# Second layer of a two-layer AdaLN model: positive parts and normalisation on ScalarE, inverse roots on GpSimd, key tiles in pairs, one output scaling per tile

## The chip, the cores and the metric

The kernel runs on one core of a Trainium2 chip. A core has TensorE (PE, matmuls), VectorE (DVE), ScalarE (ACT), GpSimd (POOL) and SyncE (SP, here only the issue of DMAs), each with an instruction queue of its own that is worked off in order. The metric is device time in microseconds (us), the median of several runs. All data are float32.

## The reference

Two layers, each an attention and a mixture of experts, both with a layer norm that is scaled and shifted per batch. x has four batches of 1024 rows of 256 columns. The change touches the second layer's attention and the routing of its experts. Cut to that:

```python
h = _layernorm(x) * (1 + ca) + sa
q, k, v = split(h @ w_qkv.T)                  # 16 heads of 16
q = norm(norm(relu(q) + 1e-6) ** 3)           # norm: t / t.sum(-1)
k = norm(norm(relu(k) + 1e-6) ** 3)
kv = einsum('bhnd,bhne->bhde', k, v)
z = 1 / (einsum('bhnd,bhd->bhn', q, k.sum(2)) + 1e-6)
out = einsum('bhnd,bhde,bhn->bhne', q, kv, z)
out = out + conv3(out) + b_dwc                # three taps along the rows
x = x + ga * (out @ w_proj.T + b_proj)
h = _layernorm(x) * (1 + cb) + sb
logits = h @ router_w + router_b              # 8 experts, the largest is taken
x = x + gb * gate * (h @ expert_w[idx] + expert_b[idx])
```

## The kernel before, in words

x stays on the chip, one tile of 128 partitions by eight row tiles by 256 columns for each batch. The first layer's attention, its experts, the second layer's attention and its experts follow one another. The second attention (`attention1`) starts while the last two batches of the first experts are still being put together (`combine`: `out` is scaled by ScalarE, gets its second term on VectorE, is multiplied by the gate on GpSimd and added to x on VectorE).

`attention1` works batch by batch. `front(b)` takes the layer norm (`layer_norm_steps`: statistics and inverse root, normalised rows `ln_xn`, transposes into `ps_lnT`, scaled and shifted into `hT`), then the keys and values: for each row tile a product `ps_k`, its positive part plus 1e-6 (`r`), the cube (`k3`, shown as k), the reciprocal of the head's sum (`recs`), and the values times that reciprocal (`v`, with the reciprocal itself as a 17th column of each head). The product `ps_kv` of k and v is issued two row tiles late, through the list `waiting`. Then four tiles of queries `ps_q` are cubed into `qT`. `back(b)` multiplies qT with the summed kv (`ps_o`), divides (`on`), transposes (`ps_oT`, `o`), applies the three taps (`y`), projects (`ps_pr`) and adds to x. The bias is added to x on GpSimd beforehand (the 128x1024 addition of `bg`).

Steps of `front(b)` and `back(b-1)` alternate, and with each step `Around` spends a credit on work beside: first `combine`, then the routing `route` of batches whose attention is done (`row_statistics`, and `routed_rows`: normalise, scale and shift into `h`, transpose, multiply with the router's weights, turn the result). Ranks and lists follow (`ps_rank`, `ps_list`), and GpSimd scatters the rows to the experts' places (`sorted`). The gate's products `scaled` for the final sum stand on GpSimd too. The last batch is routed in two halves of four tiles. In this part of the kernel a scheduler orders the instructions of each engine; the order is fixed when the kernel is built, and every engine keeps to it.

An inverse root is either `rsqrt` (13 small instructions on VectorE, three Newton steps) or `power` (an addition and a power on GpSimd).

PSUM has eight banks: three for `ps_p` (ps_k, ps_q), three for `ps_m` (ps_lnT, ps_o, ps_oT, ps_pr and the routing's), two for the sums of kv.

Of the kernel before, what the change touches and what calls it, by code (L numbers as in the profile page):

```python
# [8 lines left out]
F32 = mybir.dt.float32  # L9
# [99 lines left out]

def layer_norm_T(k, b, hT, layer, which, psum, psum_tag):  # L110
    for _ in layer_norm_steps(k, b, hT, layer, which, psum, psum_tag, k.work):
        pass


def layer_norm_steps(k, b, hT, layer, which, psum, psum_tag, xn_pool):
# [13 lines left out]
    rsqrt(nc, pool, rstd, mv[:, :, 1], NT, LN_EPS)  # L129
    yield 1.5  # L130
    for q in range(2):
        xn = xn_pool.tile([P, 4, C], F32, tag="ln_xn", name="ln_xn", bufs=k.xn_bufs)
        for i in range(4):
            t = 4 * q + i
            nc.vector.tensor_scalar(
                xn[:, i, :], k.x[b][:, t, :], mv[:, t, 0:1], rstd[:, t : t + 1],
                ALU.subtract, ALU.mult,
            )
        yield 1.5
        for cc in range(CC):  # L140
            yield BANK
            ps = psum.tile([P, 512], F32, tag=psum_tag, name="ps_lnT")
            for i in range(4):
                nc.tensor.transpose(
                    ps[:, i * P : (i + 1) * P], xn[:, i, cc * P : (cc + 1) * P], k.ident
                )
            scale = k.modT[layer][:, 6 * which + 2 + cc, b : b + 1]
            shift = k.modT[layer][:, 6 * which + cc, b : b + 1]
            dst = hT[:, cc, q * 512 : (q + 1) * 512]
            if cc == 0:  # L150
                nc.vector.tensor_scalar(dst, ps, scale, shift, ALU.mult, ALU.add)  # L151
            else:
                nc.scalar.activation(dst, ps, AF.Identity, bias=shift, scale=scale)
            yield 0.7
# [919 lines left out]
def routed_rows(k, work, b, t0, nt, h, mv, rstd, scale, shift, wr):  # L1074
# [3 lines left out]
    for q in range(0, nt, 4):  # L1078
        for i in range(q, q + 4):
            nc.vector.scalar_tensor_tensor(  # L1080
                h[:, i, :C], k.x[b][:, t0 + i], mv[:, i, 0:1], scale, ALU.subtract, ALU.mult
            )
            nc.vector.scalar_tensor_tensor(
                h[:, i, :C], h[:, i, :C], rstd[:, i : i + 1], shift, ALU.mult, ALU.add
            )
            yield 0.9
# [375 lines left out]
def attention1(ctx, k, a, after_rows=lambda b, t, n: None):  # L1462
# [6 lines left out]
    ps_p = ctx.enter_context(k.tc.tile_pool(name="a1_ps_p", bufs=3, space=PSUM, reuse_waits="tile"))  # L1469
    ps_m = ctx.enter_context(k.tc.tile_pool(name="a1_ps_m", bufs=3, space=PSUM, reuse_waits="tile"))  # L1470
# [27 lines left out]
    same = same.rearrange("p (h d) -> p h d", d=D)  # L1498
    kvs, qTs = {}, {}

    recs = wp.tile([P, 2, B, NT, H], F32, tag="recs", name="recs")

    def front(b):
# [13 lines left out]
        for t in range(NT):  # L1517
            ps = ps_p.tile([P, 512], F32, tag="p", name="ps_k")
            for cc in range(CC):
                nc.tensor.matmul(  # L1520
                    ps, lhsT=hT[:, cc, t * P : (t + 1) * P], rhs=wqkv[:, cc, C:],
                    start=cc == 0, stop=cc == CC - 1,
                )
            r = work.tile([P, C], F32, tag="r", name="r", bufs=3)
            nc.vector.tensor_scalar(r, ps[:, :C], 0.0, 1e-6, ALU.max, ALU.add)  # L1525
            k3 = work.tile([P, C], F32, tag="k3", name="k3", bufs=3)
            nc.scalar.activation(k3, r, AF.Square)  # L1527
            nc.gpsimd.tensor_tensor(k3, k3, r, ALU.mult)
            rk = recs[:, 0, b, t]
            nc.vector.tensor_reduce(rk, k3.rearrange("p (h d) -> p h d", d=D), AX.X, ALU.add)  # L1530
            nc.vector.reciprocal(rk, rk)
            v = work.tile([P, H, D + 1], F32, tag="v", name="v", bufs=3)
            nc.gpsimd.tensor_copy(v[:, :, D], rk)  # L1533
            nc.vector.tensor_tensor(  # L1534
                v[:, :, :D], ps[:, C:].rearrange("p (h d) -> p h d", d=D), bcast(rk, 2, D), ALU.mult
            )
            waiting.append((t, k3, v))
            if len(waiting) > 2:
                product(*waiting.pop(0))
            yield  # L1540

        qT = qTs[b] = work.tile([P, CC, N], F32, tag="qT", name="qT")
        for cc in range(CC):
            for q in range(2):
                cols = slice(q * 512, (q + 1) * 512)
                ps = ps_p.tile([P, 512], F32, tag="p", name="ps_q")
# [6 lines left out]
                nc.vector.tensor_scalar(r, ps, 0.0, 1e-6, ALU.max, ALU.add)  # L1553
                nc.scalar.activation(qT[:, cc, cols], r, AF.Square)
                nc.gpsimd.tensor_tensor(qT[:, cc, cols], qT[:, cc, cols], r, ALU.mult)
# [15 lines left out]
    def back(b):  # L1571
# [10 lines left out]
        for q in range(2):  # L1582
            on = work.tile([P, 4, C], F32, tag="on", name="on")
            for i in range(4):
# [9 lines left out]
                for cc in range(CC):  # L1594
                    nc.vector.tensor_tensor(
                        on[:, i, cc * P : (cc + 1) * P].rearrange("p (h d) -> p h d", d=D),
                        ps[:, cc, :P].rearrange("p (h d) -> p h d", d=D),
                        bcast(z[:, cc], 2, D), ALU.mult,
                    )
# [201 lines left out]
class Experts1:  # L1801
# [24 lines left out]
    def route(self, block):  # L1826
# [7 lines left out]
        mv, rstd = yield from row_statistics(k, self.work, b, t0, nt, rsqrt)  # L1834
# [4 lines left out]
        tr = yield from routed_rows(k, self.work, b, t0, nt, h, mv, rstd, scale, shift, self.wr)  # L1839
# [299 lines left out]
```

## Time and profile before

| | |
|---|---|
| time, median of 3 runs (lowest to highest) | 1149.53 us (1149.14 to 1150.41) |
| profiled execution: its own time, its span | 1181.49 us, 1179.8 us |
| mean granted TensorE clock of that execution | 0.897 |
| busy over the span: PE, DVE, ACT, POOL | 943.3, 642.7, 513.4, 476.8 us |
| first layer norm instruction of the second attention | about 768 us |
| first ps_k, last ps_pr of the second attention | 780.7 us, about 1038 us |
| first transpose of an expert's tile after it | 1065.5 us |

The profiled execution is one execution, with the profiler on, and takes 32 us more than the median. In the profile a line such as L1525 is a line of the kernel; a fp32 matmul shows as two records; what ends an engine's idle time is named after it. Idle time of an engine that nobody waits for costs nothing.

### The profile page before, as it was taken

Reading aid. Unit: us, or ns where it says so; the run is one execution under the profiler, and the core shown is the slowest. Engines: PE = TensorE matmul, PEld = TensorE weight load, DVE = VectorE, ACT = ScalarE, POOL = GpSimd, SP = SyncE. Lnnn points to the kernel's source line nnn. Section 1 sums busy time; section 2 is a strip of 40 time slices with the busy share of each in tenths; the row PEclk is TensorE's granted clock in tenths of the full one; section 3 lists DMA queues with packets and bytes.
Section 4 is the critical chain, followed back from the end, with each engine's and each line's share of the span. In section 5 each row is a group of like instructions: output and inputs, shape, how many; then the busy total and the mean of one; then the engine's idle time right before and its main releaser. Section 6 shows DMA issues by size and latency. Waiting matters only on the chain.

```text
span 1179.8 us, 18176 instructions
## 1 busy us (share of the span) xinstructions
PE 943.3 (80%) x5920; PEld 546.9 (46%) x5920; DVE 642.7 (54%) x1971; ACT 513.4 (44%) x777; POOL 476.8 (40%) x714
## 2 busy tenths in 40 slices
PE   5699999999999988796879989636787888646750
PEld 3443434434434433234758878413544554434640
DVE  4351336324624464324656656588895877772263
ACT  0148765776686554563546656521213131211110
POOL 0012212222542374431465556765244425443561
PEclk9789999999999998897989998767898999868875
DMA  6200000000100042317235334353001001014455
GB/s 223 81 14 2 1 1 6 5 1 1 50 33 1 10 152 99 125 56 277 90 132 173 124 100 145 109 161 125 1 5 41 1 10 40 6 59 152 148 193 170
DMA packets 62726, 92.18 MB, mean 78 GB/s; under 512 B 9170, under 2 KB 53144, under 8 KB 61857
## 3 DMA queue, kind: packets, MB, share of 16 engines
q1 hardware_dynamic: 51488, 64.88, 17.1%
q0 software_dynamic: 10272, 25.24, 6.0%
q8 instruction: 50, 0.82, 0.3%
q10 hardware_dynamic: 864, 0.82, 0.2%
q14 instruction: 52, 0.42, 0.1%
HBM read 58.02 MB, written 35.76 MB: 79 GB/s over the span
## 4 chain that ended last, share of the span: by engine, by line
PE 47%; DVE 18%; POOL 12%; issue 11%; DMA 5%; ACT 3%; SPq 1%; another core or an unknown queue 1%; DVEq 0%; POOLq 0%; ACTq 0%
PE ps_s L425 12%; PE ps_av L498 11%; POOL results L1114 5%; PE ps_q L409 3%; PE ps_out L469 2%; PE ps_pr L1625 2%; PE ps_mod L170 2%; PE ps_h L1302 2%; DMA xs<-sorted 2%; POOL sorted L1062 2%; DMA wmod<-in_wmod_dram 1%; PE ps_lat L362 1%; DMA ys<-results 1%; PE ps_lnT L1092 1%; PE ps_rows L184 1%
## 5 line engine op out<-in xcount | busy, mean ns | idle before, releaser
L433 ACT ACTIVATE pT<-ps_s 128x1024 f32<-128x1024 f32 x288 | 278.9, 1022 | 135.4 <-PE ps_s L425 121.8
L436 POOL TENSOR_SCALAR_AFFINE_SELECT pT<-pT 128x256 f32<-128x256 f32 x256 | 100.7, 415 | 282.6 <-ACT pT L433 278.2
L425 PE MATMUL ps_s<-qT,kT 32*128 32x512 f32 (+3 forms) x1536 | 178.5, 529 | 4.4 <-ACT pT L433 4.4
L498 PE MATMUL ps_av<-pT,v 128*32 128x512 f32 (+3 forms) x1536 | 168.3, 500 | 7.7 <-DVE sq L447 5.8
L1062 POOL DMA_INDIRECT sorted<-h,index x96 | 96.7, 1007 | 62.6 <-DVE ln_rstd L99 26.4
L425 PEld LDWEIGHTS ps_s<-qT,kT 32*128 32x128 f32 x1536 | 74.6, 185 | 101.5 <-issue 73.2
L1114 POOL DMA_INDIRECT results<-y,ids x79 | 80.1, 1014 | 55.3 <-DVE y L1366 38.1
L1350 ACT ACTIVATE act<-ps_hT,gain 128x128 f32<-128x128 f32 x158 | 59.4, 456 | 66.4 <-PE ps_hT L1346 52.6
L498 PEld LDWEIGHTS ps_av<-pT,v 128*32 128x32 f32 x1536 | 41.6, 109 | 98.3 <-issue 55.6
L1361 PE MATMUL ps_y<-w,act 128*128 x316 | 81.9, 405 | 1.8 <-ACT act L1350 1.8
L1302 PE MATMUL ps_h<-w,xT 128*128 x316 | 79.4, 396 | 0.6 <-issue 0.3
L447 DVE STREAM_TRANSPOSE sq<-ps_av 128x512 f32<-128x512 f32 x32 | 22.8, 713 | 100.4 <-PE ps_av L498 100.4
L1520 PE MATMUL ps_k<-wqkv,hT 128*128 128x512 f32 x128 | 70.0, 675 | 6.2 <-DVE hT L151 6.2
L1361 PEld LDWEIGHTS ps_y<-w,act 128*128 128x128 f32 x316 | 63.6, 204 | 12.7 <-ACT act L1350 3.1
L1302 PEld LDWEIGHTS ps_h<-w,xT 128*128 128x128 f32 x316 | 59.3, 198 | 9.3 <-issue 1.2
L1307 DVE TENSOR_TENSOR hid<-ps_h,b 128x256 f32<-128x256 f32 x79 | 33.5, 424 | 45.5 <-PE ps_h L1302 34.7
L1114 POOL DMA_INDIRECT results<-y,xs x39 | 38.0, 975 | 39.6 <-DVE y L1911 26.8
L1905 PE MATMUL ps_y<-we,xT 128*128 x156 | 45.3, 442 | 10.5 <-ACT xT L1900 8.2
L1334 ACT ACTIVATE hid<-hid,nmr,rstd 128x256 f32<-128x256 f32 x79 | 43.7, 611 | 11.3 <-DVE nmr L1324 11.3
L1511 PE MATMUL ps_kv<-v,k 128*128 128x136 f32 x128 | 23.0, 305 | 31.0 <-DVE v L1534 24.6
L1511 PEld LDWEIGHTS ps_kv<-v,k 128*128 128x128 f32 x128 | 19.9, 206 | 53.5 <-POOL v L1533 44.6
L1527 ACT ACTIVATE k<-r 128x256 f32<-128x256 f32 x32 | 13.3, 417 | 71.2 <-DVE r L1525 35.3
(233 smaller groups left out, 1645.0 us busy)
## 6 DMA issues: line engine op xcount, KB each, us to landing
xs<-sorted SPq DMA_DIRECT2D x118, 128.5 KB
w<-in_w_dram SPq DMA_DIRECT2D x8, 1024.0 KB
ys<-results SPq DMA_DIRECT2D x32, 256.0 KB
x<-in_x_dram SPq DMA_DIRECT2D x4, 1024.0 KB
b<-in_b_dram SPq DMA_DIRECT2D x2, 2048.0 KB
ys<-results SPq DMA_DIRECT2D x8, 512.0 KB
out_dram<-x SPq DMA_DIRECT2D x8, 512.0 KB
sorted<-fill SPq DMA_DIRECT2D x26, 128.5 KB
```

What stands on the lines that cost most here:

```text
L425: nc.tensor.matmul(pair[hh // 2][:, hh % 2, c0 : c0 + w], lhsT=kTs[o][rows, kb * P : (kb + 1) * P], rhs=qT[rows, q1 - w : q1], start=True, ...
L433: nc.scalar.activation(pT, ps, AF.Exp, scale=1.0 / L**0.5)
L436: nc.gpsimd.affine_select(out=pT[:, :, c0 : c0 + P], in_=pT[:, :, c0 : c0 + P], compare_op=ALU.is_ge, fill=0.0, base=0, pattern=[[0, 2], [ ...
L498: nc.tensor.matmul(po[32 * hh : 32 * hh + 32, 512 - w :], lhsT=vs[b % 2][:, kb, at : at + 32], rhs=exps[n, u][hh // 2][:, hh % 2, c0 : c0 ...
L1062: i = self.k.nc.gpsimd.indirect_dma_start(out=self.buffer.ap, out_offset=bass.IndirectOffsetOnAxis(ap=index, axis=0), in_=rows, in_offset= ...
L1114: k.nc.gpsimd.indirect_dma_start(out=buffer.ap, out_offset=bass.IndirectOffsetOnAxis(ap=ids, axis=0), in_=y, in_offset=None, bounds_check= ...
L1302: nc.tensor.matmul(ph[:, j], lhsT=st.xT[:, j, cc], rhs=w1[:, cc, bass.ds(st.at[j], C)], start=cc == 0, stop=cc == CC - 1,)
L1334: nc.scalar.activation(st.h[:, j], st.h[:, j], AF.Identity, bias=st.nmr[:, at : at + 1], scale=st.rstd[:, at : at + 1],)
L1350: nc.scalar.activation(st.act[:, j, cc], pt[:, j, cc], AF.Gelu, bias=gain[:, 1, cc, t : t + 1], scale=gain[:, 0, cc, t : t + 1],)
L1361: nc.tensor.matmul(po[:, j], lhsT=st.act[:, j, cc], rhs=w2[:, cc, bass.ds(st.at[j], C)], start=cc == 0, stop=cc == CC - 1,)
L1520: nc.tensor.matmul(ps, lhsT=hT[:, cc, t * P : (t + 1) * P], rhs=wqkv[:, cc, C:], start=cc == 0, stop=cc == CC - 1,)
L1905: nc.tensor.matmul(po[:, j], lhsT=xT[:, j, cc], rhs=we[:, cc, bass.ds(at[j], C)], start=cc == 0, stop=cc == CC - 1,)
```

## The change

- The second layer's layer norm: `power` on GpSimd in place of `rsqrt` on VectorE. The rows are normalised by ScalarE (`normal_rows`: a small product `nmr` of minus the mean and the root on VectorE, then one Identity with scale and bias for each row tile). All of hT is written by ScalarE.
- The routing: the same root and the same `normal_rows`, then for four row tiles together a product with the scale on VectorE and an addition of the shift on GpSimd.
- Keys: two row tiles share one two-bank PSUM tile. The positive part (Relu), the addition of 1e-6 (Identity with the bias `tiny`) and the square are three ScalarE instructions, the last product stays on GpSimd (`cubed`). Sum, reciprocal and values are one instruction each for the pair, and the reciprocal is copied into v by ScalarE. Queries use `cubed` too.
- `on`: one product for a row tile's 16 heads in place of two.
- PSUM: `ps_p` has two tiles of two banks, `ps_m` two of one bank.

```diff
+def normal_rows(k, pool, dst, x, mv, root):
+    nmr = pool.tile([P, n], F32, tag="ln_nmr", name="ln_nmr")
+    nc.vector.scalar_tensor_tensor(nmr, mv[:, :, 0], -1.0, root, ALU.mult, ALU.mult)
+    for t in range(n):
+        nc.scalar.activation(
+            dst[:, t, :C], x[:, t], AF.Identity, bias=nmr[:, t : t + 1], scale=root[:, t : t + 1]
+        )
...
-    rsqrt(nc, pool, rstd, mv[:, :, 1], NT, LN_EPS)
+    if layer:
+        power(nc, k, pool, rstd, mv[:, :, 1], NT, LN_EPS)
+    else:
+        rsqrt(nc, pool, rstd, mv[:, :, 1], NT, LN_EPS)
...
+        if layer:
+            ts = slice(4 * q, 4 * q + 4)
+            normal_rows(k, pool, xn, k.x[b][:, ts], mv[:, ts], rstd[:, ts])
...
-            if cc == 0:
+            if cc == 0 and not layer:
                 nc.vector.tensor_scalar(dst, ps, scale, shift, ALU.mult, ALU.add)
...
+        if layer:
+            four = h[:, q : q + 4, :C]
+            normal_rows(
+                k, work, four, k.x[b][:, t0 + q : t0 + q + 4], mv[:, q : q + 4], rstd[:, q : q + 4]
+            )
+            yield 1
+            nc.vector.tensor_tensor(four, four, bcast(scale, 1, 4), ALU.mult)
+            yield 1
+            nc.gpsimd.tensor_tensor(four, four, bcast(shift, 1, 4), ALU.add)
+            yield 1
...
-    ps_p = ctx.enter_context(k.tc.tile_pool(name="a1_ps_p", bufs=3, space=PSUM, reuse_waits="tile"))
-    ps_m = ctx.enter_context(k.tc.tile_pool(name="a1_ps_m", bufs=3, space=PSUM, reuse_waits="tile"))
+    ps_p = ctx.enter_context(k.tc.tile_pool(name="a1_ps_p", bufs=2, space=PSUM, reuse_waits="tile"))
+    ps_m = ctx.enter_context(k.tc.tile_pool(name="a1_ps_m", bufs=2, space=PSUM, reuse_waits="tile"))
...
+    def cubed(dst, ps, r):
+        nc.scalar.activation(r, ps, AF.Relu)
+        nc.scalar.activation(r, r, AF.Identity, bias=tiny)
+        nc.scalar.activation(dst, r, AF.Square)
+        nc.gpsimd.tensor_tensor(dst, dst, r, ALU.mult)
...
-        for t in range(NT):
-            ps = ps_p.tile([P, 512], F32, tag="p", name="ps_k")
...
-            nc.vector.tensor_scalar(r, ps[:, :C], 0.0, 1e-6, ALU.max, ALU.add)
-            nc.scalar.activation(k3, r, AF.Square)
-            nc.gpsimd.tensor_tensor(k3, k3, r, ALU.mult)
...
+        for t in range(0, NT, 2):
+            ps = ps_p.tile([P, 2, 512], F32, tag="p", name="ps_k")
...
+            cubed(k3, ps[:, :, :C], r)
+            rk = recs[:, 0, b, t : t + 2]
+            nc.vector.tensor_reduce(rk, k3.rearrange("p i (h d) -> p i h d", d=D), AX.X, ALU.add)
             nc.vector.reciprocal(rk, rk)
...
-            nc.gpsimd.tensor_copy(v[:, :, D], rk)
+            nc.scalar.copy(v[:, :, :, D], rk)
...
-                nc.vector.tensor_scalar(r, ps, 0.0, 1e-6, ALU.max, ALU.add)
-                nc.scalar.activation(qT[:, cc, cols], r, AF.Square)
-                nc.gpsimd.tensor_tensor(qT[:, cc, cols], qT[:, cc, cols], r, ALU.mult)
+                cubed(qT[:, cc, cols], ps, r)
...
-                for cc in range(CC):
-                    nc.vector.tensor_tensor(
-                        on[:, i, cc * P : (cc + 1) * P].rearrange("p (h d) -> p h d", d=D),
-                        ps[:, cc, :P].rearrange("p (h d) -> p h d", d=D),
-                        bcast(z[:, cc], 2, D), ALU.mult,
-                    )
+                nc.vector.tensor_tensor(
+                    on[:, i].rearrange("p (c h d) -> p c h d", c=CC, d=D),
+                    ps[:, :, :P].rearrange("p c (h d) -> p c h d", d=D), bcast(z, 3, D), ALU.mult,
+                )
...
-        mv, rstd = yield from row_statistics(k, self.work, b, t0, nt, rsqrt)
+        mv, rstd = yield from row_statistics(k, self.work, b, t0, nt, power)
```

## The prediction

> **What bounds the kernel now.** I read the page's slices first, to find the second layer's attention, then busy time by stretch, then what TensorE waited for, then groups and single instructions.
>
> ```profile
> PE   5699999999999988796879989636787888646750
> DVE  4351336324624464324656656588895877772263
> ACT  0148765776686554563546656521213131211110
> POOL 0012212222542374431465556765244425443561
> PEclk9789999999999998897989998767898999868875
> ```
> A slice is 29.5 us. The change acts from slice 26 to 35 (767 to 1065 us): there VectorE shows 8 and 9, ScalarE 1 to 3, TensorE 6 to 8 after a slice of 3. Cut where the last ps_oT of each batch ends:
>
> ```profile
> 767.00:846.00 79.00, 43.98 (x148) 25.51 (x148) 67.50 (x226) 16.11 (x34) 41.55 (x58) 0.73 0.32 106
> 846.00:904.00 58.00, 48.03 (x224) 30.15 (x223) 46.49 (x147) 14.80 (x25) 23.70 (x32) 0.94 0.05 12
> 904.00:961.00 57.00, 46.32 (x179) 28.05 (x177) 43.21 (x128) 11.92 (x20) 22.86 (x32) 0.91 0.05 16
> 961.00:1019.00 58.00, 47.39 (x230) 29.13 (x229) 42.54 (x139) 14.45 (x26) 27.95 (x37) 0.97 0.07 24
> 1019.00:1065.00 46.00, 18.91 (x116) 13.91 (x116) 32.56 (x128) 6.82 (x12) 13.20 (x14) 0.63 0.13 43
> ```
> Columns: length, then busy PE, PEld, DVE, ACT, POOL, the granted clock, DMA. I call these stretches b0, b1, b2, b3 and the tail. In b0 VectorE is busy 67.5 of 79 us and bounds. In b1 to b3 TensorE is busy 46 to 48 of 58: only some 10 us a batch are left to win, and VectorE at 43 to 46 is not far behind. So what counts is latency: how long TensorE's in-order queue stands in front of a product.
>
> ```profile
> PE ps_k L1520 <- DVE hT L151: 4.3, 1, 4.3
> PE ps_kv L1511 <- DVE v L1534: 3.2, 4, 2.0
> PE ps_kv L1511 <- DVE rs_a L97: 1.3, 1, 1.3
> ```
> These waits of b2 (us in total, times, longest) show it: the products ps_kv wait for the chain ps_k, r, k, recs, v. In b1 the first one waits 1.97 us and then tiles run every 2.18 us (ps_k at 865.00, 867.18, 869.36), which is TensorE's own pace.
>
> ```profile
> L1528 POOL TENSOR_TENSOR k<-k,r 128x256 f32<-128x256 f32 x32 | 24.6, 769 | 29.7 <-ACT k L1527 29.7
> L1555 POOL TENSOR_TENSOR qT<-qT,rq 128x512 f32<-128x512 f32 x16 | 21.1, 1321 | 14.4 <-ACT qT L1554 14.4
> L1083 DVE SCALAR_TENSOR_TENSOR h<-h,ln_rstd,shift_f 128x256 f32<-128x256 f32 x32 | 19.0, 618 | 0.0
> L1530 DVE TENSOR_REDUCE recs<-k 128x16 f32<-128x256 f32 x32 | 13.3, 416 | 15.2 <-POOL k L1528 15.0
> L1554 ACT ACTIVATE qT<-rq 128x512 f32<-128x512 f32 x16 | 10.1, 630 | 28.7 <-DVE rq L1553 24.8 <-DVE rs_a L96 4.0
> ```
> The second number after the bar is the mean in ns: prices of the new forms come from here. ScalarE sits idle before its steps and nobody waits long for it: it has room, but each step put there lengthens a chain.
>
> **What the Trainium skill says.** "SBUF — State Buffer", section "SBUF: two separate sides": a VectorE instruction with two SBUF inputs and a GpSimd one that reads SBUF exclude each other for the whole instruction. The trace agrees:
>
> ```profile
> 876.98 2.52 POOL L1610 TENSOR_TENSOR x<-x,bg 128x1024 f32<-128x1024 f32 x1
> ```
> Beside it one L1083, mean 0.62, took 2.23 us (877.56). "ScalarE: Activation LUTs", section "What ACT_TABLE_LOAD costs": 186 ns, 0.833 ns per element, 93 ns more for each per-partition operand, 93 ns of overlap back to back. The trace agrees: L1334 with two such operands and 256 elements took 0.61 (0.585 by the rule), L1442 with one 0.50 (0.49). Section "Table sets: the hidden batching unit" of that page: relu and identity are in every set; the stage loads one table (L1846, 1.28 us), for its Exp, so no new load is expected. "TensorE: Matmul & The Clock Gate", section "What's actually happening": an idle TensorE falls to half clock and needs a busy stretch to recover. After 7.26 us of idling, 16 ps_pr records took 6.42 us, where 30 took 6.64 us in b1.
>
> **The change part by part.** Busy time first, 767 to 1065 us. VectorE loses r 12.9, rq 10.7, ln_xn 14.4, hT 6.4, the routing's two steps L1080 and L1083 33.8, and nine roots of 13 instructions (91 of eight columns add to 21.5, 26 of four at 0.15 make 3.9): 103.6. It gains 16 small nmr at 0.15 and eight 128x1024 products at 1.23 (L547 has that shape): 12.2. Merging gives recs 13.3 to 16x0.68, reciprocals 7.6 to 16x0.25, v 13.2 to 16x0.68, on 14.0 to 32x0.41: 9.1 less. Net 100 off 232.
> ScalarE gains 32 Relu at 0.63 (20.2), 32 additions of tiny, one operand, 512 elements, 0.71 by the rule (22.7), 64 normalisations at 0.61 (39.2), eight hT at 0.775 (6.2), 16 copies into v at 0.2 (3.3), and the merged squares give back 3.2: 88 onto 64.
> GpSimd gains nine roots. L107 took 1.04 for four columns and 0.89 for three, so 1.66 for eight, and 0.23 for the addition of eps: 1.9, in all 16. It gains eight additions of shift, 2.36 each as L1610: 19; it loses the copies, 6.9, and 3.5 by merging. Net 24 onto 129. TensorE and SyncE have the same instructions; no moved step issues a DMA. No engine becomes the bound by its sum (VectorE 132, ScalarE 152, GpSimd 153, TensorE 205), so the end is set by the order in the queues, which I read from the built program.
>
> b1, from the end of ps_pr (A; 859.05 before). Before, the first ps_kv starts at A+5.4, after 1.97 us of waiting. After: the last statistics end about A+2.0 (A+2.9 before, with other work between); the root takes 1.9 and two hand-offs 0.2; nmr 0.15: A+4.3. ScalarE's queue then holds h, relu, h, +tiny, h, square: three h at 0.52, then 0.54, 0.62, 0.63: A+7.7. The pair's relu thus stands behind an h that waits for all eight tiles' statistics, though its ps_k ended near A+1.5. GpSimd's product 1.32 and a hand-off: A+9.1. On VectorE recs 0.68, then the routing's product h 1.23 queued ahead, reciprocal 0.25, v 0.68, hand-offs: A+12.0. TensorE has eight transposes (1.2) and five ps_k (2.5 tiles at 1.72, 4.3) to do: it idles 6.5 instead of 1.97. **+4.5.** In b1 alone one transpose of h stands ahead of that ps_kv; it waits for GpSimd's addition, A+11.1+2.4: **+1.6.** The first hT, before on VectorE, now sits behind y (1.24) in ScalarE's queue: ps_k waits 2.5 instead of 0.9, **+1.6** (b2's wait of 4.3 there, of unclear origin, I leave). Later pairs: relu, +tiny, square 1.8 after overlap, product 1.32, recs, reciprocal, v 1.6, hand-offs 0.4: 5.1 against 4.3 that TensorE has to do: +0.5 a batch, and a 2.4 us addition in GpSimd's queue is paid from slack. The 2.1 us wait behind the blocked L1083 goes: -2.0. on is 0.49 to 0.41: -0.6. b1: **+5.6**. b2: 4.5+0.5, qT one step longer 0.5, on -0.6, smaller waits gone -0.9: **+4.0**. b3: 4.5+1.6+0.5, less 2.0 as the routing's matmuls fill the hole, -1.1 for the rest: **+3.5**.
>
> b0: in 803 to 827 tiles took 3.2 us against 2.18 of TensorE, VectorE being the cause: up to 8.2 to win. But the third pair's product on GpSimd stands behind the root of x3, due only after the last combine: I give back 3.2. **-5.0** (0 to -9). The first layer norm's root, 5.1 us on VectorE before, takes 2, but ScalarE does all four rows, and the first `out` on GpSimd stands behind the second root: 0.
>
> Tail: the rank of batch 2 stands on VectorE behind an nmr whose root waits on GpSimd behind an addition (2.4) and a scaled (1.9): +2.0 before the twelve scatters (-2 to +5).
>
> The smaller pools, three buffers to two in each: the third ps_pr waits for the first addition to x (0.68), 0 to +2 a batch; I take 0, the queue covers it. Unknown costs: the eight-column root 1.3 to 2.5; tiny 0.6 to 0.8; a collision on the shared port -1 to +2.5 each.
>
> Sum -5.0+5.6+4.0+3.5+2.0 = **+10.1** against the profiled execution (1181.5 us, span 1179.8). The median is 1149.5, 0.973 of that: +9.8, about **1159**.
>
> **Rivals.** (1) Faster. VectorE's relief shortens what TensorE waits for it: 33, 9, 10 and 7 us in b0 to b3. It loses 43%: 25 us, less 10 for longer chains: -15, **1134**. For it: the first row of stretches. Against: waits are latency, not queue, from b1 on. It decides if the relu of the first pair starts within 2 us of its ps_k and the first ps_kv idles under 3 us. (2) Equal: b0 and the tail give 10 and the batches take 10, **1149.5**. (3) Slower by more: each addition of shift collides with a product or y on VectorE (eight times 1.2) and the idle holes halve TensorE's clock: +20, **1169**. That ScalarE doesn't take the work isn't possible; that it hides there is rival 1.
>
> **How the numbers follow.** 0.2% is 2.3 us, about what a measurement of this kernel can tell from no change. Forecast 0.40, rival 3 0.15, rival 2 0.08, rival 1 0.37. Hence slower 0.55, same 0.08, faster 0.37. The likeliest case alone spans 1151 to 1167 by its bounds; both signs hold much, so the range goes from 1128 (rival 1 and its unknowns) to 1172.
>
> **What would show it.** Right: after each ps_pr in b1 to b3 a wait of 5 us or more ahead of the first ps_kv; VectorE near 132 us busy, ScalarE near 152; b1 near 64 us long, b0 near 74; roots on GpSimd near 1.9. Wrong: that wait under 3 us, b0 shorter by over 9, or a batch under 56.

## The result, and the profile after

The changed kernel takes 1188.07 us (median of four, 1186.35 to 1190.31) against 1149.55 for the kernel before in the same session: 1.0335 of it, 95% interval 1.0315 to 1.0356, or 38.5 us more. Slower was the likelier side of the forecast, but +10 was a quarter of what came. The slices of the page after:

```profile
PE   5699999999999988878799978536788776654760
DVE  4351346334623655345756656583536354552363
ACT  0158765875686466545556656353463634411110
PEclk9799999999999999997999989667888899866885
```

In the stage (slices 26 to 34, counted from 0) VectorE shows an 8 once, in b0, and then 3 to 6. Before, it showed 7 to 9 in all slices of the stage but one (the prediction read this as 8 and 9). ScalarE has 3 to 6 where it had 1 to 3, and TensorE is no fuller. Every engine waits.

The profile shown ahead of the prediction was some 34 us longer than a second one of the same kernel (29 us outside this stage, 5.6 in b2), and the runs of one session stood at that level throughout, so lengths below are compared with the second profile, and each ratio with runs of the kernel before in the same session. The stretches, cut as in the prediction but with b0 starting at the first statistics; first the second profile of the kernel before, then the changed kernel:

```profile
753.60:831.10 77.50, 43.61 (x146) 25.41 (x147) 66.81 (x222) 15.72 (x33) 40.36 (x46) 0.73 0.31 105
831.10:890.10 59.00, 48.99 (x230) 30.82 (x229) 46.99 (x149) 15.41 (x27) 24.28 (x32) 0.94 0.04 14
890.10:941.30 51.20, 41.76 (x179) 25.82 (x178) 43.18 (x127) 11.85 (x21) 22.52 (x32) 1.00 0.05 16
941.30:999.30 58.00, 47.04 (x228) 29.02 (x226) 42.52 (x139) 14.10 (x26) 27.37 (x37) 0.97 0.07 24
999.30:1046.10 46.80, 17.32 (x116) 12.75 (x117) 32.97 (x128) 6.94 (x12) 14.40 (x14) 0.72 0.14 45
```

```profile
750.00:833.40 83.40, 44.79 (x144) 25.26 (x144) 50.20 (x128) 34.80 (x67) 45.61 (x42) 0.71 0.29 98
833.40:902.40 69.00, 52.51 (x228) 33.31 (x228) 31.04 (x80) 34.20 (x61) 28.85 (x26) 0.85 0.05 15
902.40:960.50 58.10, 43.56 (x176) 27.11 (x176) 26.32 (x60) 30.77 (x55) 24.18 (x22) 0.94 0.04 11
960.50:1028.60 68.10, 50.26 (x228) 30.82 (x228) 34.10 (x81) 29.02 (x52) 25.44 (x25) 0.95 0.06 20
1028.60:1082.40 53.80, 19.92 (x118) 14.45 (x118) 29.45 (x89) 10.89 (x20) 27.02 (x23) 0.61 0.12 40
```

All five stretches are longer: +5.9, +10.0, +6.9, +10.1 and about +7, together some 40 us, which is the whole result. In b1 to b3, 168.2 us before and 195.2 after, two things grew by the first two columns: TensorE's idle time from 30.4 to 48.9 us, and its busy time from 137.8 to 146.3 us. The work is the same, but the granted clock was 0.85, 0.94 and 0.95 against 0.94, 1.00 and 0.97. So about a third of these 27 us is no wait, but slower matmuls. No run tries this apart, and busy time varies by itself: `on_only` below, as fast as the kernel before, has 141.4 us of it.

What TensorE waited for from b1 to b3, first before, then after:

```profile
PE ps_kv L1511 <- DVE v L1534: 11.0, 7, 3.7
PE ps_pr L1625 <- DVE y L1617: 5.2, 3, 1.7
```

```profile
PE ps_kv L1548 <- DVE v L1570: 13.2, 4, 6.5
PE ps_lnT L1121 <- POOL h L1106: 7.6, 1, 7.6
PE ps_k L1558 <- ACT hT L172: 4.9, 3, 1.6
PE ps_kv L1548 <- ACT r L1533: 3.6, 1, 3.6
```

These are the longest entries. All waits of ps_kv together went from 15.9 only to 18.3 us; the rest grew by the routing's h, by hT and by many small ones.

And the groups of the chain after, with the idle time ahead of them:

```profile
L1566 DVE TENSOR_REDUCE recs<-k 128x32 f32<-128x512 f32 x16 | 10.9, 683 | 46.1 <-POOL k L1536 46.1
L1569 ACT COPY v<-recs 128x32 f32<-128x32 f32 x16 | 3.9, 243 | 37.0 <-DVE recs L1567 37.0
```

VectorE stood 46 us for GpSimd's product and ScalarE 37 us for VectorE's reciprocals. The work was moved to engines that had room; what grew is the chain from ps_k over ScalarE, GpSimd and VectorE to ps_kv.

### The profile page after: what moved, and what is told of

Read it like the earlier page. It is cut to its first block, busy times and chain, and to the rows that moved or that the text cites. A ratio compares the mean times of both kernels' runs of the same rounds, so it can differ in the third digit from the quotient of the medians.

```text
span 1185.3 us, 17939 instructions
## 1 busy us (share of the span) xinstructions
PE 937.5 (79%) x5920; PEld 544.8 (46%) x5920; DVE 582.0 (49%) x1646; ACT 589.2 (50%) x913; POOL 500.5 (42%) x693
## 5 line engine op out<-in xcount | busy, mean ns | idle before, releaser
L444 PE MATMUL ps_s<-qT,kT 32*128 32x512 f32 (+3 forms) x1536 | 176.0, 527 | 0.6 <-ACT pT L452 0.6
L1558 PE MATMUL ps_k<-wqkv,hT 128*128 128x512 f32 x128 | 67.4, 661 | 4.9 <-ACT hT L172 4.9
L1548 PE MATMUL ps_kv<-v,k 128*128 128x136 f32 x128 | 23.5, 340 | 46.4 <-DVE v L1570 41.3
L1939 PE MATMUL ps_y<-we,xT 128*128 x156 | 42.7, 422 | 2.0 <-ACT xT L1934 1.0
L1659 PE MATMUL ps_pr<-wg,y 128*128 128x256 f32 x128 | 33.0, 408 | 7.6 <-DVE y L1651 5.7
```

The costliest lines, as they stand in the source:

```text
L444: nc.tensor.matmul(pair[hh // 2][:, hh % 2, c0 : c0 + w], lhsT=kTs[o][rows, kb * P : (kb + 1) * P], rhs=qT[rows, q1 - w : q1], start=True, ...
L1558: nc.tensor.matmul(ps[:, i], lhsT=hT[:, cc, (t + i) * P : (t + i + 1) * P], rhs=wqkv[:, cc, C:], start=cc == 0, stop=cc == CC - 1,)
L1659: nc.tensor.matmul(pt[:, i, :], lhsT=y[:, cc, (t + i) * P : (t + i + 1) * P], rhs=wg[:, cc, :], start=cc == 0, stop=cc == CC - 1,)
L1939: nc.tensor.matmul(po[:, j], lhsT=xT[:, j, cc], rhs=we[:, cc, bass.ds(at[j], C)], start=cc == 0, stop=cc == CC - 1,)
```

## The experiments

One table first. Ratios are against the kernel before in the same session; the stretches, from one profiled execution each, are differences to the second profile of the kernel before (us). A single stretch is good to one or two us; b2 of the kernel before alone differed by 5.6 between two profiles. For `ln_rows_only`, `v_gpsimd`, `single_tiles` and `best1`, whose session stood at the first profile's level, the five differences add to 4 to 7 us more than the ratio gives, so their b2 above all is to be read with care. An edit also changes the order in which the scheduler puts the instructions around it; what is called the cost of a part includes that. "Kv loop" is the time from the start of a batch's first ps_kv to the end of its last, and "query step" the time from there to the end of its last ps_oT. In the expectations, "blind working" is the prediction.

| kernel | ratio (95%) | b0 | b1 | b2 | b3 | tail |
|---|---|---|---|---|---|---|
| changed | 1.0335 (1.0315 to 1.0356) | +5.9 | +10.0 | +6.9 | +10.1 | +6.8 |
| no_rows | 1.0184 (1.0156 to 1.0212) | +1.2 | +5.7 | +8.6 | +12.5 | -2.1 |
| no_route | 1.0262 (1.0213 to 1.0311) | +5.9 | +6.9 | +10.6 | +7.3 | -2.0 |
| no_key | 1.0167 (1.0138 to 1.0196) | -2.5 | +5.3 | +4.6 | +4.8 | +5.8 |
| on_only | 1.0001 (0.9987 to 1.0015) | +0.1 | +0.8 | +1.2 | 0.0 | -0.1 |
| roots_only | 0.9988 (0.9974 to 1.0001) | -7.1 | -0.5 | +1.3 | +2.1 | +4.2 |
| cubed_only | 0.9959 (0.9946 to 0.9971) | -3.5 | -1.8 | +0.2 | -0.7 | +0.6 |
| pairs_only | 1.0122 (1.0088 to 1.0156) | +1.0 | +5.8 | +7.2 | +5.5 | -1.3 |
| psum_only | 1.0149 (1.0120 to 1.0177) | +3.3 | +6.7 | +6.1 | +5.8 | -1.7 |
| two_key_buffers | 1.0127 (1.0097 to 1.0158) | +1.4 | +4.2 | +6.8 | +4.3 | -0.2 |
| ln_rows_only | 1.0026 (1.0004 to 1.0047) | -2.3 | +4.3 | +3.9 | +1.3 | +0.2 |
| hT_only | 0.9995 (0.9981 to 1.0010) | -2.2 | +0.9 | +1.0 | +1.4 | +0.2 |
| route_rows_only | 1.0133 (1.0106 to 1.0160) | -1.3 | +1.8 | +2.8 | +4.3 | +5.6 |
| v_gpsimd | 1.0307 (1.0254 to 1.0359) | +3.3 | +9.0 | +10.5 | +10.9 | +6.5 |
| single_tiles | 1.0173 (1.0124 to 1.0223) | -1.7 | +9.2 | +6.6 | +7.5 | +5.5 |
| k_vector | 1.0280 (1.0252 to 1.0307) | +3.0 | +8.3 | +7.5 | +6.1 | +6.3 |
| best1 | 0.9934 (0.9914 to 0.9953) | -3.5 | -1.4 | +1.8 | -0.6 | +0.6 |
| best2 | 0.9946 (0.9925 to 0.9966) | -2.7 | -2.3 | -1.2 | -0.7 | -0.5 |

### The kernel before once more

> The kernel before, unchanged, profiled once more: its first profiled execution took 1181.5 us where the median is 1149.5. Theory: the extra 32 us lie outside the stretches b0 to b3 and the tail (18 us of it before them, 12 to 14 after the first ps_xT), so that these stretches come out again at 77.4 (counted from the first statistics), 58.9, 56.8, 57.5 and 46.7 us, within 1 us each, the second attention starting near 750 us. Rival: the extra lies in the stretches as well; then one of them comes out over 3 us shorter.

No edit. The stretches came out at 77.5, 59.0, 51.2, 58.0 and 46.9 us, starting at 753.6. Four stretches came out as the theory had them. b2 was 5.6 us shorter, as the rival said of one stretch: where ps_k had waited 4.35 us ("of unclear origin" in the prediction) and six of its records then took 5.49 us, it waited 0.91 and they took 2.84, and the kv loop was 1.2 us shorter.

### Half of the change undone

`no_rows`: `layer_norm_steps` and the routing take the path of the first layer again (`rsqrt`, rows and half of hT on VectorE).

```diff
-        mv, rstd = yield from row_statistics(k, self.work, b, t0, nt, power)
+        mv, rstd = yield from row_statistics(k, self.work, b, t0, nt, rsqrt)
...
-        tr = yield from routed_rows(k, self.work, b, t0, nt, h, mv, rstd, scale, shift, self.wr, 1)
+        tr = yield from routed_rows(k, self.work, b, t0, nt, h, mv, rstd, scale, shift, self.wr)
...
-    if layer:
+    if False:
```

> The changed kernel with the whole normalisation put back as before: layer norm and routing rows on VectorE, inverse roots on VectorE, hT shared by VectorE and ScalarE. Key pairs, ScalarE's relu and the merged output scaling stay. Theory (two halves: a serial chain for each pair of key tiles with two PSUM pairs, and rows whose normalisation queues ahead of it): tail back to about 47, first ps_kv some 7 us after the end of ps_pr, later pairs still above 4.6 us each: near 1168. Rival A (the pair chain is nearly all of it): above 1178. Rival B (the rows are nearly all of it, as the blind working had it): below 1158.

`no_route`: the first two edits of these alone.

> The changed kernel with only the routing's rows and their roots back on VectorE; layer norm, roots and rows of the attention stay on GpSimd and ScalarE, key pairs stay. Theory: the tail's 7 us return and the relu of the first pair loses the h ahead of it, 3 to 4 us in each of b1 to b3: near 1170. Rival A: above 1178. Rival B: below 1160.

`no_key`: the key and query loops and the PSUM pools of the kernel before.

```diff
-        for t in range(0, NT, 2):
+        for t in range(NT):
...
-            cubed(k3, ps[:, :, :C], r)
+            nc.vector.tensor_scalar(r, ps[:, :C], 0.0, 1e-6, ALU.max, ALU.add)
+            nc.scalar.activation(k3, r, AF.Square)
+            nc.gpsimd.tensor_tensor(k3, k3, r, ALU.mult)
...
-    ps_p = ctx.enter_context(k.tc.tile_pool(name="a1_ps_p", bufs=2, space=PSUM, reuse_waits="tile"))
+    ps_p = ctx.enter_context(k.tc.tile_pool(name="a1_ps_p", bufs=3, space=PSUM, reuse_waits="tile"))
```

> The changed kernel with the key and query steps back as before: single tiles, positive part by one VectorE step, copy into v on GpSimd, three PSUM buffers in each pool. Normalisation by ScalarE, roots by GpSimd and the merged output scaling stay. Theory: tiles run at 2.2 us again, but squares stand behind h on ScalarE and the tail keeps its 7 us: near 1170. Rival A: below 1160. Rival B: above 1180.

Measured: 1171.66, 1180.42 and 1169.99 us, against 1151.23 in that session. With either half gone some 19 to 21 us stay, as the theory said of `no_rows` and `no_key`, and neither rival. `no_route` missed: it took 8 us off (1.0262 against 1.0335), not 18, and fell where rival A had it (above 1178), with an interval of 1174 to 1185. The tail returned (-2.0 against before), b1 to b3 hardly. The reason is in b1 of `no_route`, after ps_pr ended at 851.0:

```profile
853.44 0.59 ACT L117 ACTIVATE ln_xn<-x,ln_nmr,ln_rstd 128x256 f32<-128x256 f32 x1
853.93 0.58 ACT L1533 ACTIVATE r<-ps_k 128x512 f32<-128x512 f32 x1
857.94 2.33 POOL L1644 TENSOR_TENSOR x<-x,bg 128x1024 f32<-128x1024 f32 x1
858.04 2.52 DVE L1112 SCALAR_TENSOR_TENSOR h<-h,ln_rstd,shift_f 128x256 f32<-128x256 f32 x1
863.28 2.15 PE L1548 MATMUL ps_kv<-v,k 128*128 128x136 f32 x8
```

With the routing's rows away from ScalarE, the next layer norm's rows stand there between the steps of the first pair, and on VectorE a routing step that GpSimd's addition stretches to 2.5 us. The first ps_kv still comes 12.3 us after ps_pr (13.0 in the changed kernel).

### One part alone on the kernel before

`on_only` has the merged `on`; `roots_only` has `power` for `rsqrt` in both places; `cubed_only` has `cubed` in the key loop, tile by tile, and in the query loop; `pairs_only` has the pair loop with

```diff
-            cubed(k3, ps[:, :, :C], r)
+            nc.vector.tensor_scalar(r, ps[:, :, :C], 0.0, 1e-6, ALU.max, ALU.add)
+            nc.scalar.activation(k3, r, AF.Square)
+            nc.gpsimd.tensor_tensor(k3, k3, r, ALU.mult)
...
-            nc.scalar.copy(v[:, :, :, D], rk)
+            nc.gpsimd.tensor_copy(v[:, :, :, D], rk)
```

> The kernel before with the merged output scaling alone. Theory: in b1 to b3 TensorE and not the scaling sets the pace from the last ps_kv to ps_oT (with the key loop undone that stretch took 19.2, 12.1, 12.0 us against 19.3, 12.3, 12.2), in b0 it went from 17.2 to 13.2, but there the rest of the normalisation may have done it: 1146 to 1149, about -1 against before. Rival (the blind working's 0.6 a batch in b1 to b3 and nothing in b0): -2.

1151.01 us, ratio 1.0001: nothing, not even the expected 1 us.

> The kernel before with only the inverse roots of the second layer by GpSimd (layer norm and routing), the rows still on VectorE. Theory: VectorE loses 117 small steps and gains no wait worth naming in b1 to b3; in the tail the root queues behind the two scaled steps on GpSimd and the rank stands behind it: tail +2 to +5, the rest -3 to +1: 1147 to 1153, about 1150. Rival (the tail's 7 us come from the rows by ScalarE and from nmr, not from the root): tail within 1 us of 46.9.

1151.06 us, 0.9988. The theory held in the total and in the tail, which lost 4.2 (51.1 us, so the rival fell). b0 won 7.1, more than expected, and b1 to b3 lost 2.9.

> The kernel before with positive part, addition and square by ScalarE for single key tiles and for the query quarters; three PSUM buffers and GpSimd's copy stay. Theory: key tiles keep TensorE's pace (1.3 us of ScalarE for 2.2 of TensorE), the query step costs 2 to 2.6 us a batch as in the changed kernel, since its relu stands behind square and copy of the one before: 1149.5 + 9 = about 1158. Rival (with three PSUM buffers the query step hides it): 1147 to 1152.

1145.95 us, 0.9959: faster by 4.7, and below the rival too. The forecast cost of the query step did not show: from the last ps_kv to the last ps_oT b1 to b3 took 19.3, 12.8 and 12.8 us against 19.3, 12.3 and 12.2.

> The kernel before with key tiles two at a time and two PSUM buffers in each pool; positive part by one VectorE step, copy into v by GpSimd. Theory: the chain of a pair is longer than that of a tile and only two pairs fit: first ps_kv 2 to 3 us later in b1 to b3, tiles a little over TensorE's pace, the burst of scatters in b3 no longer covered: +12 to +16, about 1163. Rival (ScalarE's three steps and its copy make the chain slow, not the pairs): under 1154.

1166.06 us, 1.0122, 14 us. As expected in size; but the edit has two parts in it, and the next two runs part them.

### The PSUM buffers

`psum_only` sets both pools of the kernel before to `bufs=2`, `two_key_buffers` only `a1_ps_p`:

```diff
-    ps_p = ctx.enter_context(k.tc.tile_pool(name="a1_ps_p", bufs=3, space=PSUM, reuse_waits="tile"))
+    ps_p = ctx.enter_context(k.tc.tile_pool(name="a1_ps_p", bufs=2, space=PSUM, reuse_waits="tile"))
```

> The kernel before with two buffers instead of three in each of the two PSUM pools, and single key tiles as before. Theory (the pairing itself costs, since a pair's chain starts only when both tiles are done and holds both banks to its end): 0 to +4. Rival (the third buffer is what was lost): +10 to +14, as with pairs.

> The kernel before with two PSUM buffers for key and query tiles instead of three; the other pool keeps its three. Theory (a key tile's bank is held until its v is written, so with two of them every other ps_k waits for the v of the tile before): the key loop 4 to 5 us longer in each of b1 to b3, +11 to +14 of the 17 us that both pools cost. Rival (the other pool, where ps_pr, ps_lnT, ps_o and ps_oT share): 0 to +5.

1168.23 and 1164.95 us: 1.0149 and 1.0127. The theory of `psum_only` fell and that of `two_key_buffers` held: on the kernel before, nearly all of the cost is the third buffer of the key tiles. The main wait of TensorE from b1 to b3 in `two_key_buffers` (the kernel before has no wait of ps_k on v in its list):

```profile
PE ps_k L1520 <- DVE v L1534: 12.9, 7, 3.7
```

and TensorE in b1 of `psum_only`:

```profile
852.10 0.63 PE L1511 MATMUL ps_kv<-v,k 128*128 128x136 f32 x4
854.54 1.96 PE L1520 MATMUL ps_k<-wqkv,hT 128*128 128x512 f32 x4 [1.82 <-DVE v L1534]
856.33 0.63 PE L1511 MATMUL ps_kv<-v,k 128*128 128x136 f32 x4
856.79 1.94 PE L1520 MATMUL ps_k<-wqkv,hT 128*128 128x512 f32 x4
858.57 0.63 PE L1511 MATMUL ps_kv<-v,k 128*128 128x136 f32 x4
860.87 1.96 PE L1520 MATMUL ps_k<-wqkv,hT 128*128 128x512 f32 x4 [1.67 <-DVE rs_a L96]
```

Of these three ps_k the first and the last wait 1.8 and 1.7 us for a bank, the one between them doesn't: a tile's bank is held from its ps_k until v, which reads the second half of it, is written (the small rs_a named once ended 0.07 us after a v, the next in VectorE's queue).

Pairs with two times two banks cost the same within the intervals (1.0122), but the wait looks different. In the list of `pairs_only`, as in that of the changed kernel, no ps_k waits for v. Instead ps_kv does (13.8 us, 5 times, from b1 to b3): with pairs it stands ahead of the next ps_k in TensorE's queue and waits for the same v. So it isn't shown whether, with pairs, the banks or the product issued only one pair late set the pace. Three pairs were not tried; they would take all six banks that the sums of kv leave.

### The rows, part by part

`ln_rows_only` and `route_rows_only` put the layer norm's or the routing's part of the change on the kernel before; `hT_only` only this:

```diff
-            if cc == 0:
+            if cc == 0 and not layer:
```

> The kernel before with the layer norm's part of the change alone: its inverse root by GpSimd, its rows and all of hT by ScalarE; routing as before. Theory: of the 18 us that all rows cost, hT behind y in ScalarE's queue makes 2 us a batch from ps_oT to the end of ps_pr, b0 wins 2 to 5: +1 to +4, near 1154. Rival (these rows are the costly ones): above 1160.

1184.46 us against 1181.56: 1.0026, as expected.

> The kernel before with all of the second layer's hT by ScalarE and nothing else. Theory (a step of the blind working: the first hT now stands behind y in ScalarE's queue): from the last ps_oT to the end of ps_pr 1.6 to 2 us more in b1 to b3, as with the layer norm's part alone (15.2, 16.0, 17.8 against 13.5, 13.5, 16.0): +4 to +6. Rival: ps_k has other work ahead of it and nothing is seen: within 1 us.

1151.05 us, 0.9995. The step is there: from the last ps_oT to the end of ps_pr b1 took 15.4 us (13.5 before) and b3 17.8 (16.0), b2 13.7 (13.5). ps_k waited 2.3 us for hT in each of the three, 0.9 before. But b0 won 2.2, and the total shows nothing.

> The kernel before with the routing's part of the change alone: its roots and its additions of shift by GpSimd, its rows normalised by ScalarE, the product with scale on VectorE. Theory: the layer norm's part alone cost 3 us and both together 18.6, so the routing's is the larger: tail +6, and 2 to 4 us in each of b1 to b3 from GpSimd's eight additions in front of key products: +12 to +15 against before. Rival (it is the meeting of both parts on ScalarE that costs): +5 to +8, nearly all in the tail.

1165.77 us, 1.0133, 15 us: the larger part of the rows, as expected; 5.6 of it in the tail. The share of GpSimd's additions was not tried alone.

### Where the parts meet

Multiplied, the parts alone (0.9959, 1.0122, 1.0026, 1.0133, 1.0001) make 1.0242, 27.8 us; 10.7 of the 38.5 are interplay. Rows together (`no_key`, 1.0167) are the product of their two halves (1.0159). Pairs and ScalarE's positive part together (`no_rows`, 1.0184) are not: 1.0082, 11.7 us short.

`v_gpsimd`, on the changed kernel:

```diff
-            nc.scalar.copy(v[:, :, :, D], rk)
+            nc.gpsimd.tensor_copy(v[:, :, :, D], rk)
```

> The changed kernel with the copy of the reciprocals into v on GpSimd, as before; nothing else. Pairs alone cost 14.3 us and ScalarE's positive part alone wins 4.7, but both together (with the merged scaling) cost 21: 12 us of interplay. Theory: it is ScalarE's own copy into v, which waits for the reciprocals of a pair and holds the relu of the next pair behind it, so that pairs run one after the other: 1178 to 1182. Rival: two PSUM pairs are the limit whichever engine copies: within 3 us of 1188.

1.0307 against 1.0335 of the changed kernel, some 3 us, and the intervals overlap. The middle of the interval, 1185, is nearer to the rival, but its lower end reaches into the theory's range. The copy that waits on ScalarE (37 us in the list above) most likely holds up little that the pairs would not.

`single_tiles`: the changed kernel with `for t in range(NT)`, one tile in each bank and three buffers.

> The changed kernel with key tiles one at a time and three PSUM buffers in each pool; everything else as changed, ScalarE's positive part and copy into v included. Theory: the pairs' own cost and their interplay with ScalarE go, the rows' 18 us stay, less 4 that ScalarE's positive part wins: 1162 to 1167. Rival (relu and h crowd each other on ScalarE whatever the tiles): above 1174.

1.0173, which of 1149.55 is 1169: some 19 below the changed kernel, a little above the theory's range and short of the rival's; its interval, 1164 to 1175, touches both. In b1 it has the kv loop at 24.3 us, where `cubed_only` has 18.5 and the kernel before 20.8: with the rows on ScalarE, its three steps (and its copy into v) no longer win 4.7 us, they win nothing (`no_key`, without them: 1.0167). At the middle of the intervals relu and rows thus crowd each other by some 5 us, but the intervals allow none, so this isn't shown.

`k_vector`: the changed kernel with the product of the key tiles on VectorE.

```diff
+    def cubed(dst, ps, r, mul=nc.gpsimd):
...
+        mul.tensor_tensor(dst, dst, r, ALU.mult)
...
+            cubed(k3, ps[:, :, :C], r, nc.vector)
```

> The changed kernel with the last product of the key tiles on VectorE instead of GpSimd; the query's stays. Theory (GpSimd's queue costs b3 and b0 their excess: eight scatters, 10 us, or two roots in front of a product that ps_kv waits for): b3 6 to 8 us shorter, b0 4 to 6, the other batches 0 to 2 each: 12 to 16 us below the changed kernel, +22 to +26 against before. Rival (the pair's chain on ScalarE and the two buffers set the pace anyway): less than 5 us below it.

1.0280: 6 us below the changed kernel, half of the theory's least, and little more than the rival's most. What it removes is this, in b3 of the changed kernel:

```profile
992.72 1.10 POOL L1081 DMA_INDIRECT sorted<-h,index  x1 [0.17 <-DVE whole L986]
1001.83 0.97 POOL L1081 DMA_INDIRECT sorted<-h,index  x1 [0.31 <-issue]
1002.81 1.29 POOL L1536 TENSOR_TENSOR k<-k,r 128x512 f32<-128x512 f32 x1
1004.13 0.69 DVE L1566 TENSOR_REDUCE recs<-k 128x32 f32<-128x512 f32 x1 [8.84 <-POOL k L1536]
1006.14 2.15 PE L1548 MATMUL ps_kv<-v,k 128*128 128x136 f32 x8 [4.43 <-DVE v L1570]
```

Eight scatters, 10.1 us from first to last end, in front of the third pair's product. b3 became 4.0 shorter and b0 2.9.

### Two versions built from the parts that won

`best1` is `cubed_only` with `power` for the layer norm's root; `best2` is `cubed_only` with the key tiles' last product on VectorE.

> The kernel before with two parts of the change that did not cost: positive part, addition and square by ScalarE on single tiles, and the layer norm's inverse root by GpSimd (the routing's root stays on VectorE, since GpSimd's cost 4 us in the tail). Theory: 4.7 from the first, and of the 7 us that roots won in b0 some 3 that do not overlap with it: 1141 to 1144, tail at 47. Rival (GpSimd's root lost in b1 to b3 what it won in b0): 1146, as with the first part alone.

1172.43 against 1181.56: 0.9934, as expected. But the stretches do not show what was to bring it: b0, where the root was to win, is -3.5, as with `cubed_only` alone.

> The kernel before with positive part, addition and square by ScalarE on single tiles (alone 0.996 of before) and the key tiles' last product on VectorE instead of GpSimd. Theory: the product leaves the queue in which scatters and roots stand, and takes less time on VectorE: a further 2 to 5 us, 0.992 to 0.994 of before. Rival (VectorE, which ScalarE's steps had relieved, is full again in b0): 0.996 or more.

1143.13 against 1150.15: 0.9946, between theory and rival; the kv loop is a little shorter in b0 to b2 (22.3, 18.0, 17.7 us against 23.5, 18.5, 19.3 in `cubed_only`). Both beat the kernel before and the changed one. The intervals of the three (0.9959, 0.9934, 0.9946) overlap, so which addition helps, if either, stays open.

## Why the prediction was right or wrong

The sum was +10.1, and by stretch it missed 10.9 us in b0, 4.4, 2.9 and 6.6 in b1 to b3, and 4.8 in the tail. Two terms that it put at nothing failed, the smaller pools and the delay of the combine in b0; a third, the tail, was too small.

**The smaller pools, costed at 0 (0 to 2 a batch): the step that failed most clearly.** Measured +14.7 us for the key tiles' pool alone (1.0127), +17 for both, +14 for pairs with their pools; single tiles with three buffers took some 19 off the changed kernel. The working looked at the pool of ps_pr, where it was right about the wait: with both pools reduced, ps_pr waits for x 2.2 us in three waits of up to 1.0, and from ps_oT to the end of ps_pr b2 and b3 took 15.1 and 18.2 us, against 13.5 and 16.0 before and with the key pool alone reduced. It did not ask how long a key tile holds its bank. The trace of before answers that: in b1 of its second profile ps_k of a tile starts at 850.51 and its v ends at 856.20, 5.7 us. An estimate from this: three buffers give 3 x 2.18 = 6.5, enough; two give one tile per 2.85, 0.67 more for each of eight tiles, 5.4 a batch. Measured from the end of ps_pr to the last ps_kv in `two_key_buffers`: +5.3, +6.8 and +4.3 in b1 to b3. So close a fit is in part luck, since the next tiles of b1 held their banks 6.2 to 9.5 us. In `pairs_only` a pair, with its longer chain, held its banks 9.7 to 15 us in b1 to b3, from the second of a batch on.

The Trainium skill's "Perfetto Trace Analysis", section "Optimization Strategy", says that the same gap repeating on the engine that should be full can mean that the next tile has no SBUF or PSUM to go to. The waits of ps_k for v in `two_key_buffers` and `psum_only` are that; this case adds that the reserve can be estimated before it is spent.

**The first ps_kv at A+12.0: right, and for the order in the queues that was read; but taking that order away did not help.** Measured 13.0, 11.6 and 10.9 us after the end of ps_pr (before 5.4, 5.4, 4.0). In b1 h stands ahead of the relu, and one transpose of h ahead of ps_kv; 7.57 us of idling against 6.5 and 1.6 forecast:

```profile
852.73 0.60 ACT L117 ACTIVATE h<-x,ln_nmr,ln_rstd 128x256 f32<-128x256 f32 x1 [1.49 <-DVE ln_nmr L115]
853.24 0.58 ACT L1533 ACTIVATE r<-ps_k 128x512 f32<-128x512 f32 x1
861.42 0.47 PE L1121 MATMUL ps_lnT<-ident,h 128*128 128x128 f32 x1 [7.57 <-POOL h L1106]
861.69 2.02 PE L1548 MATMUL ps_kv<-v,k 128*128 128x136 f32 x8
```

Without the routing's rows (`no_route`) ps_kv comes at 4.2 in b3, but still at 12.3 in b1 and b2, where the rows of the layer norm then stand in that place. The three parts that `no_route` keeps give for b1, each alone, +2.9 (pairs), +0.6 (ScalarE's steps) and +3.3 (layer norm), which with 5.4 make 12.2.

**hT behind y, +1.6 in b1 and b3: right alone, half of it in the changed kernel.** In `hT_only` ps_k waits 2.3 us as forecast (2.5), and from the last ps_oT to the end of ps_pr it takes +1.9 and +1.8 (b2 +0.2), but b0 pays it back. In the changed kernel ps_k waits 1.6 us for hT in each of b1 to b3, 0.7 more than before.

**b0, forecast -5.0, came out +5.9.** VectorE's relief can win there: roots alone win 7.1, ScalarE's steps 3.5, all rows 2.5. Two buffers take 3.3 (`psum_only`). The working had 8.2 to win in the kv loop and gave 3.2 back, since the third pair's product stands behind the root of x3, due after the last combine. The product does stand there, but when the combine ends was put at no change (the first `out` behind the second root: 0). It ended 47.2 us after the first statistics instead of 39.2, and the first `out` on GpSimd came 3.4 us later. The last addition of the combine before, then what follows it after:

```profile
792.13 0.69 DVE L1453 TENSOR_TENSOR x<-x,out 128x512 f32<-128x512 f32 x1 [0.32 <-POOL out L1451]
```

```profile
794.35 2.82 DVE L1482 TENSOR_TENSOR x<-x,out 128x512 f32<-128x512 f32 x1 [0.31 <-POOL out L1480]
804.11 1.67 POOL L107 TENSOR_TENSOR ln_rstd<-rs_a,halves 128x8 f32<-128x8 f32 x1
805.74 1.26 POOL L1536 TENSOR_TENSOR k<-k,r 128x512 f32<-128x512 f32 x1
809.05 2.15 PE L1548 MATMUL ps_kv<-v,k 128*128 128x136 f32 x8 [8.14 <-DVE v L1570]
```

The kv loop took 28.7 us instead of 23.3. With the layer norm's part alone the combine ends late too (44.6), but there all key products but the last stand ahead of the roots of x2 and x3, and b0 is 2.3 shorter. The key and query steps without the rows give +1.2 (`no_rows`), the rows without them -2.5 (`no_key`): the loss comes from both together. The product's place in GpSimd's queue is not all of it: with it on VectorE (`k_vector`) b0 was only 2.9 shorter. What delays the combine was not tried apart.

**The tail, +2.0: right mechanism, mis-sized, +6.8.** The rank stood behind nmr and its root behind an addition and a `scaled`, as forecast. First the kernel before (first profile), then the changed one:

```profile
1012.38 7.45 POOL L1961 TENSOR_TENSOR scaled<-gate_f,part 128x1024 f32<-128x1024 f32 x4
1043.19 0.69 PE L933 MATMUL ps_rank<-sel,before 128*128 128x64 f32 x2 [3.32 <-DVE sel L808]
```

```profile
1045.07 3.74 POOL L1995 TENSOR_TENSOR scaled<-gate_f,part 128x1024 f32<-128x1024 f32 x2
1045.12 1.86 DVE L115 SCALAR_TENSOR_TENSOR ln_nmr<-ln_mv,ln_rstd 128x4 f32<-128x4 f32 x1 [1.49 <-POOL ln_rstd L107]
1054.61 1.05 POOL L107 TENSOR_TENSOR ln_rstd<-rs_a,halves 128x4 f32<-128x4 f32 x1
1055.62 1.91 POOL L1995 TENSOR_TENSOR scaled<-gate_f,part 128x1024 f32<-128x1024 f32 x1
1055.69 1.85 DVE L115 SCALAR_TENSOR_TENSOR ln_nmr<-ln_mv,ln_rstd 128x4 f32<-128x4 f32 x1 [3.74 <-POOL ln_rstd L107]
1059.41 0.69 PE L952 MATMUL ps_rank<-sel,before 128*128 128x64 f32 x2 [7.24 <-DVE sel L827]
```

The first root keeps all four `scaled` behind it; before, GpSimd was done with them by 1020 us (the end of ps_pr, A, was at 1037.8) and then idled 26 us. Released by the root together with nmr, a `scaled` then runs beside each nmr, and a product on 128x4 elements takes 1.86 us where its kind took 0.15. nmr reads two operands from SBUF and `scaled` reads SBUF too: the exclusion of the two engines, which the prediction cited for another pair of steps, was not applied to this one. The rank came 12.6 us after ps_pr, 5.4 before. `roots_only` shows 4.2 of the 6.8 without any row on ScalarE.

**Credits not paid.** The merged `on`, -0.6 a batch, gave 0 (`on_only`). The -2.0 in b1 for the blocked L1083 can't be told from the rest: the kv loop of b1 is 2.1 us shorter, but by the working the late start of ps_kv gives back as much (6.6 later, 4.5 lost). The -2.0 in b3 for a filled hole does not show. There the scatters stand ahead of a product instead, unforeseen.

**The query step, +0.5 in b2 and nothing in the others, took 2.1 to 2.7 more.** With both pools reduced and nothing else it takes 1.3 to 1.7 more, with the key pool alone reduced 0 or less, and with ScalarE's steps alone 0 to 0.6. So the smaller pools can make most of it: the other pool, which was not tried alone, or both together.

**Busy sums.** The root of eight columns took 1.67 and 0.24, the 1.9 that was forecast; page totals moved by +76 us for ScalarE (forecast +88) and +24 for GpSimd (+24). No table load came in: ScalarE has one in the stage, 1.28 us, as before. VectorE fell by 61 us in the stretches, not 100. The subtraction mixed two counts: a stretch counts overlapping instructions once, a group's busy time counts each in full. By groups VectorE went from 274 to 187 us, -88; most of the missing 12 is nmr (7.7 us, not 2.4) and steps of the combine that took longer (the two of `out` and x, some 5 us).

**The rivals.** Rival 1 asked for a relu within 2 us of its ps_k and less than 3 us of idling: not seen. Rival 3 named the sign and half of the size. Its collisions are there (in the tail), and TensorE's clock fell, but to 0.85 to 0.95 in b1 to b3 as a whole, with 8.5 us more of busy time, a term that the forecast itself did not have.

**Left open:** 11.7 us of interplay between pairs and ScalarE's steps. By the middle of the intervals, ScalarE's copy is some 3 us of it; putting k's product on VectorE won 6. Most of the difference between `no_rows` and `pairs_only` lies in b3 (12.5 against 5.5), where the first ps_kv comes 10.1 us after ps_pr instead of 4.2; this was not tried apart.

## What to carry to other kernels

Before giving a PSUM bank away, read from the trace how long a tile holds it, from its matmul to the last reader, and divide by the buffers: where that is above the pace of the loop, expect to pay the difference for every tile. Where a root or a product is said to wait for other work, ask whether the change moves the end of that work too. In these runs, moving steps off a busy engine gained most where that engine was the bound (b0); in b1 to b3 each hop and each in-order queue that the chain was led through could cost, and the step in front of it was at times one that has nothing to do with it. Try the parts of a change alone: here one of five was worth keeping, and it was hidden under the cost of the rest.

## What was not expected of the hardware

- A VectorE product on 128x4 elements took 1.86 and 1.85 us when it started within 0.07 us of a GpSimd `scaled` of 1.9 us; twelve of its sixteen took 0.15 to 0.17 us.
